# Routing groups in four classes: one half-width group, one shared condition, last stores behind it

## The chip, the cores and the metric

The kernel runs on one core of a Trainium2 chip. The core has a matrix engine (TensorE, "PE" in the profile, its weight loads "PEld"), a vector engine (VectorE, "DVE"), an activation engine (ScalarE, "ACT"), a general engine (GpSimd, "POOL") and a synchronisation engine (SyncE, "SP") that issues most transfers. Each engine runs its own list of instructions in order and waits on semaphores for the others. The metric is the device time of one execution in microseconds, the median of several; lower is better. Before the change it is 1043.65 us (three runs, 1042.89 to 1044.31).

## What is computed

There are 128 batches of 64 rows of 256 numbers. Each batch has a type label from 0 to 2 (of five experts) and goes through the dense layer of its own expert and through two shared ones; a softmax gate weighs the three results, and a diffusion step follows.

```python
def _dense(x, wi_, wo_):
    return jax.nn.relu(x @ wi_) @ wo_
x = hidden_states                                   # (128, 64, 256)
s0 = _dense(x, swi[0], swo[0])
s1 = _dense(x, swi[1], swo[1])
h = jax.nn.relu(jnp.einsum('bsd,bdf->bsf', x, wi[type_label]))   # 256 -> 1024
eo = jnp.einsum('bsf,bfd->bsd', h, wo[type_label])               # 1024 -> 256
gate_in = jnp.concatenate([eo[:, 0], s0[:, 0], s1[:, 0]], axis=-1)
w = jax.nn.softmax(jax.nn.relu(gate_in @ g1) @ g2, axis=-1)[:, :, None, None]
x = x + eo * w[:, 0] + s0 * w[:, 1] + s1 * w[:, 2]
x = x + diffusion(x, zX, zY, zR)
```

## The kernel before

**Stages.** The kernel runs two long items with the shared layers (about 0 to 90 us), five items that each take sixteen batches of one expert ("fours"), then a stage of smaller groups of batches of one expert, and then the rest of the shared layers with gate and diffusion. `stream` (L979) is the stage of smaller groups. Only this stage, the ordering of the batches ahead of it, and the seam behind it are touched.

**Groups.** `order_batches` (L256) sorts the batches on the chip by expert: small VectorE operations count them and cut each expert's count into pieces of 16, 8 and 4 batches. `GROUPS` lists the smaller ones: four groups of eight batches (512 columns) and seven of four (256 columns). The first nine (`NRUN`) always run. The last two stand under a condition each (`tc.If`, L1104), which compares the number of used slots, read from the table `tab`, with the slot at which the group starts. The labels of this input occur 43, 50 and 35 times, which fills 132 slots when each expert is rounded up to four.

**A group.** Each group loads its expert's weights (four transfers of 512 KB, tiles `gwr`) and its batches (64 KB each, `gxr`). `split_group_w` (L446) splits each eighth of the weights into a high part (ScalarE copy) and a low part (VectorE subtraction, `gw`); `split_group_x` (L438) does the same with the batches (low part on GpSimd, `gxl`). `up` (L894) multiplies: for each of eight slices f, six matmuls of the float32r type whose moving operand is as wide as the group (512 or 256 columns), each with its own weight load; then ScalarE writes the high part `gh` and VectorE the low part. `down` (L908) accumulates the second layer: for each block of 128 columns of the group and each f one matmul of 512 columns and one of 256. `store_group` (L926) adds the two halves of an accumulator (ScalarE, then VectorE, tile `ge`) and stores it to `eo_d`. For the last of the nine the store is issued on GpSimd's queue, otherwise on SyncE's.

**Order.** `ahead` (L938) places, before each slice f of group g, what belongs to later groups: their loads, their splits, the reloads `load_wo`. TensorE and SyncE keep the order in which the program is written; on ScalarE, VectorE and GpSimd a scheduler sets the order in this stage, and it is fixed once the program is built. Behind the stage the order is as written again (`in_order(True)`, L1160).

**Buffers.** Weights and wide tiles come from a pool of 25 slots (`pool4`), narrow ones from 16 (`small`), accumulators from 6 PSUM slots (`ppool`).

## Time and profile before

| what | us |
|---|---|
| median of the runs | 1043.65 |
| the profiled execution, time | 1042.87 |
| its span in the trace | 1040.7 |
| stage of the smaller groups (first `up` to the end of the last `gacc`) | 299.75 to 444.81 |
| first matmul behind the conditions | 446.55 |

The profile comes from one execution; what is counted out below is set against its span of 1040.7 us, and 2.2 us lie around that span. The median of the runs is 0.8 us above this execution's time. In the lines that follow, a matmul's duration contains its run through the array, so several in a row overlap; the distance from one to the next is (duration of the row less duration of one) divided by (count less one). "L88" is the helper that records each matmul, "L103" the helper that records each operation of VectorE, ScalarE and GpSimd, "L114" SyncE's transfers, "L1104" the condition.

### The profile page before, as it was taken

To read this page: it belongs to the slowest core of one execution; us is meant where nothing else is said; L and a number is where in the kernel's file an instruction comes from. 1 tells how busy PE (TensorE), PEld (TensorE's weight loads), DVE (VectorE), ACT (ScalarE), POOL (GpSimd) and SP (SyncE) were. 2 spreads that over 40 slices of the span, in tenths; PEclk is the share of its full clock that TensorE was granted. 3 is DMA by queue.
4 is the path that set the end of the run, shared out by engine and by line. 5 is a ranking of instruction groups with operands and counts; after the bars stand their busy time and mean duration, and the time that the engine had idled before them with its cause. 6 is when DMAs were issued, how large, how long until landed. Compare 5 with 4: busy or idle time off the path is not lost.

```text
span 1040.7 us, 15721 instructions
## 1 busy us (share of the span) xinstructions
PE 1031.7 (99%) x5439; PEld 884.7 (85%) x5439; DVE 810.3 (78%) x1492; ACT 572.5 (55%) x1081; POOL 154.4 (15%) x167
## 2 busy tenths in 40 slices
PE   9999999999999999999999999999999999999998
PEld 6888888888888889978888888888888888888888
DVE  7888987978777657847889778678688688688776
ACT  6476766766765546643644545446355364355362
POOL 2000000000022001211432220212212202022020
PEclk9999999999999999999999999999999999999999
DMA  6486232231457956555435435334344163253321
GB/s 217 178 280 234 76 112 86 95 122 52 132 192 235 320 174 213 183 183 219 156 128 177 135 111 200 122 122 167 111 167 156 66 224 122 81 192 140 115 77 47
DMA packets 67282, 159.14 MB, mean 153 GB/s; under 512 B 7712, under 2 KB 34848, under 8 KB 67200
## 3 DMA queue, kind: packets, MB, share of 16 engines
q1 hardware_dynamic: 64576, 149.19, 41.9%
q0 software_dynamic: 2480, 8.78, 2.4%
q8 instruction: 44, 0.72, 0.3%
q14 instruction: 38, 0.31, 0.1%
q10 hardware_dynamic: 144, 0.13, 0.0%
HBM read 126.88 MB, written 31.20 MB: 152 GB/s over the span
## 4 chain that ended last, share of the span: by engine, by line
PE 56%; DVE 1%; issue 0%; ACT 0%; DVEq 0%; ACTq 0%
PE acc L88 30%; PE pb L88 11%; PE pa L88 7%; PE pd L88 7%; PE pu L88 1%; DVE lq L103 0%; PE lin_b L88 0%; PE pgs L88 0%; PE lin_c L88 0%; PE pge L88 0%; DVE h_3a L103 0%; DVE c L103 0%; ACT u L103 0%; DVE pd L103 0%; DVE h_2b L103 0%
## 5 line engine op out<-in xcount | busy, mean ns | idle before, releaser
L88 PE MATMUL pb<-x,wi 128*128 128x512 f32 x729 | 207.9, 393 | 0.7 <-ACT pb L103 0.5
L103 ACT ACTIVATE u<-pb 128x512 f32<-128x512 f32 x162 | 96.8, 597 | 111.3 <-PE pb L88 109.7
L88 PEld LDWEIGHTS pb<-x,wi 128*128 128x128 f32 x729 | 130.4, 189 | 25.8 <-ACT u L103 2.4
L88 PE MATMUL pa<-x,wi 128*128 128x512 f32 x486 | 137.1, 390 | 1.7 <-DVEq L1104 1.7
L88 PE MATMUL pd<-x,wi 128*128 128x512 f32 x486 | 137.7, 392 | 0.4 <-DVE c L103 0.4
L103 DVE SCALAR_TENSOR_TENSOR yb<-acc,wgt,yb 128x256 f32<-128x256 f32 x216 | 99.2, 482 | 18.1 <-PE acc L88 14.4
L103 ACT ACTIVATE pb<-pa 128x512 f32<-128x512 f32 x81 | 47.2, 582 | 118.0 <-PE pa L88 117.0
L88 PEld LDWEIGHTS pd<-x,wi 128*128 128x128 f32 x486 | 90.9, 188 | 21.7 <-DVE c L103 1.6
L88 PEld LDWEIGHTS pa<-x,wi 128*128 128x128 f32 x486 | 89.9, 188 | 19.8 <-DVEq L1104 1.9
L103 DVE TENSOR_TENSOR c<-pd,u 128x512 f32<-128x512 f32 x81 | 55.9, 690 | 43.9 <-ACT u L103 32.7
L88 PE MATMUL up<-gxh,gw 128*128 128x256 f32 (+1 forms) x288 | 74.0, 331 | 0.0
L103 POOL TENSOR_TENSOR la<-yb 128x508 f32<-128x508 f32 (+1 forms) x28 | 32.1, 1148 | 260.9 <-ACT yb L103 259.4
L88 PE MATMUL gacc<-gw,gh 128*128 128x512 f32 (+1 forms) x288 | 62.7, 360 | 0.0
L103 ACT ACTIVATE gh<-up 128x256 fp32r<-128x256 f32 (+1 forms) x72 | 34.2, 477 | 42.9 <-PE up L88 42.0
L88 PEld LDWEIGHTS gacc<-gw,gh 128*128 128x128 f32 x288 | 49.9, 188 | 8.4
L88 PE MATMUL acc<-wo,h_6b 128*128 128x256 f32 (+1 forms) x172 | 56.7, 334 | 0.0
L88 PE MATMUL acc<-wo,h_1b 128*128 128x256 f32 (+1 forms) x172 | 56.7, 333 | 0.0
L88 PE MATMUL acc<-wo,h_7b 128*128 128x256 f32 (+1 forms) x172 | 56.6, 333 | 0.0
L88 PE MATMUL acc<-wo,h_0b 128*128 128x256 f32 (+1 forms) x172 | 56.5, 333 | 0.1
L88 PE MATMUL acc<-wo,h_2b 128*128 128x256 f32 (+1 forms) x172 | 56.6, 333 | 0.0
L88 PE MATMUL acc<-wo,h_3b 128*128 128x256 f32 (+1 forms) x172 | 56.5, 332 | 0.0
L88 PE MATMUL acc<-wo,h_4b 128*128 128x256 f32 (+1 forms) x172 | 56.5, 332 | 0.0
(251 smaller groups left out, 2476.2 us busy)
## 6 DMA issues: line engine op xcount, KB each, us to landing
wi<-wi_d SPq DMA_DIRECT2D x55, 896.0 KB, 4.6
gwr<-we_in SPq DMA_DIRECT2D x32, 512.0 KB, 5.3
wsr<-we_in SPq DMA_DIRECT2D x20, 512.0 KB, 5.5
xr<-xs_in SPq DMA_DIRECT2D x32, 256.0 KB, 5.1
yb<-xn_in SPq DMA_DIRECT2D x16, 512.0 KB, 5.9
y_out<-lq SPq DMA_DIRECT2D x30, 256.0 KB, 2.0
wi_d<-wi SPq DMA_DIRECT2D x8, 896.0 KB, 4.0
xr<-xg_in SPq DMA_DIRECT2D x80, 64.0 KB, 1.9
```

Of the source, the lines that this page charges most:

```text
L88: nc.tensor.matmul(out_ap, lhsT=lhsT, rhs=rhs, start=start, stop=stop, skip_group_check=True)
L103: ins = call(*args, **kwargs)
```

## The change

The order has four classes. Between the pieces of eight and of four it puts those pieces of four whose batches are sure to be more than two (count plus one, rounded down to four), and last the pieces that may hold only one or two batches. Of the last class the first unit (slots 128 and 129) runs at half width, two batches, as group number 3, between the third and the fourth group of eight; four units of four follow as before. The units 32 to 34 stand under one condition for all (used slots less four, or the end of the third class, over 128) and share their tiles. The stores of the last group that always runs move behind the condition, and to SyncE's queue. The half group has weights of its own to load; those of the fourth group of eight are loaded from slice 6 of the third on, and `load_wo` is spread over groups 0, 1 and 2 (3, 3 and 2).

```diff
+HALF = NBIG - 1
+UH = 2 * NPAIR + NSURE - 1
+GROUPS = [(2 * NB * g, 2 * NB) for g in range(2 * NQUAD, NPAIR)] + [(u * NB, NB) for u in range(2 * NPAIR, UH)]
+GROUPS.insert(HALF, (UH * NB, NB // 2))
+NRUN = len(GROUPS)
+GROUPS += [(u * NB, NB) for u in range(UH, NU)]
...
+        vec.tensor_scalar(cnt, pm[:, NE : 2 * NE], float(NB // 2 - 1), None, ALU.add)
+        vec.tensor_scalar(cnt, cnt, -NB, None, ALU.bitwise_and)
+        vec.tensor_copy(upto[:, 2, :], cnt)
+        vec.tensor_tensor(upto[:, 2, :], upto[:, 2, :], upto[:, 1, :], ALU.max)
...
-        for i in range(3):
+        for i in range(4):
             vec.tensor_add(rank, rank, shift[:, i, :])
...
-        vec.tensor_tensor(ge[0], ge[0], ge[1], ALU.min)
-        vec.tensor_tensor(tab[:, NSLOT : NSLOT + NU], ge[0], ge[2], ALU.min)
-        vec.tensor_copy(tab[:, NSLOT + NU :], base[0:1, 3 * NE :])
+        for i in range(1, 3):
+            vec.tensor_tensor(ge[0], ge[0], ge[i], ALU.min)
+        vec.tensor_tensor(tab[:, NSLOT : NSLOT + NU], ge[0], ge[3], ALU.min)
+        vec.tensor_scalar(gt[:, 0:1], base[0:1, 4 * NE :], float(-NB), None, ALU.add)
+        vec.tensor_tensor(tab[:, NSLOT + NU :], gt[:, 0:1], base[0:1, 3 * NE : 3 * NE + 1], ALU.max)
...
+    def own(g, key, make):
+        if g < NRUN:
+            return make()
+        if key not in spare:
+            spare[key] = make()
+        return spare[key]
...
-            if fs[-1] == NF - 1:
+            if fs[-1] == NF - 1 and g != NRUN - 1:
                 store_group(g, i)
...
-        if g == NRUN - 1:
-            tc.keep_in_program_order(nc.gpsimd.dma_start(rows, o))
-        else:
-            dma(rows, o)
+        dma(eo_d.rearrange("r (s d) -> (r s) d", d=D)[r0 : r0 + P, :], o)
...
             if g + 1 < NRUN:
-                if g < NBIG:
+                if g <= NBIG and g != HALF:
                     load_group_w(g + 1)
-                load_group_x(g + 1)
+                if g != HALF:
+                    load_group_x(g + 1)
             if g < 2:
                 reload(g)
-            elif g < 4:
-                for u in range(NQ):
-                    load_wo((g - 2) * NQ + u)
+            for u in range(3 * g, min(3 * g + 3, 2 * NQ)):
+                load_wo(u)
...
-        if f == 6 and NBIG <= g + 1 < NRUN - 1:
+        if g + 1 == HALF and f == 4:
+            load_group_x(g + 2)
+        if f == 6 and (g + 1 == HALF or NBIG <= g < NRUN - 2):
             load_group_w(g + 2)
...
+        if g == HALF + 1 and f + 6 < NF:
+            split_group_w(g, f + 6)
         if g + 1 < NRUN:
-            if f == 4:
+            if f == (0 if g == HALF else 4):
                 split_group_x(g + 1)
-            split_group_w(g + 1, f)
+            if g != HALF or f < 6:
+                split_group_w(g + 1, f)
...
-    for g in range(NRUN, NG):
-        with tc.If(total[0] > GROUPS[g][0]):
+    with tc.If(total[0] > UH * NB):
+        for g in range(NRUN, NG):
             load_group(g)
...
             stream(g, g + 1)
+    in_order(True)
+    for i in range(len(gacc[NRUN - 1])):
+        store_group(NRUN - 1, i)
```

More of the change, by code (lines that the diff above doesn't have):

```diff
@@ L28 @@
 NSURE = B // NB + 1 - 2 * NPAIR
-GROUPS = [(2 * NB * g, 2 * NB) for g in range(2 * NQUAD, NPAIR)] + [(u * NB, NB) for u in range(2 * NPAIR, NU)]
+HALF = NBIG - 1
[4 more added lines that the diff above has]
+GROUPS += [(u * NB, NB) for u in range(UH, NU)]
 NG = len(GROUPS)
-NRUN = NBIG + NSURE
 ST = 4
@@ L264, in order_batches @@
         gps.memset(ones, 1.0)
-        tables = slot2("tables")
-        below, part = (
-            tables[:, i * 9 * NE * NE : (i + 1) * 9 * NE * NE].rearrange("p (a b) -> p a b", b=3 * NE) for i in range(2)
-        )
+        tables = slot2("below"), slot2("part")
+        below, part = (t[:, 0 : 16 * NE * NE].rearrange("p (a b) -> p a b", b=4 * NE) for t in tables)
         gps.memset(below, 1.0)
         gps.affine_select(
-            out=below, in_=below, compare_op=ALU.is_ge, fill=0.0, base=0, pattern=[[1, 3 * NE], [-1, 3 * NE]],
+            out=below, in_=below, compare_op=ALU.is_ge, fill=0.0, base=0, pattern=[[1, 4 * NE], [-1, 4 * NE]],
             channel_multiplier=0,
@@ L296, in order_batches @@
         vec.tensor_scalar(cntb, cnt, -NB, None, ALU.bitwise_and)
-        size = const.tile([P, 3, NE], F32, name="size")
-        upto = const.tile([P, 3, NE], F32, name="upto")
-        vec.tensor_copy(upto[:, 2, :], cntb)
+        size = const.tile([P, 4, NE], F32, name="size")
+        upto = const.tile([P, 4, NE], F32, name="upto")
+        vec.tensor_copy(upto[:, 3, :], cntb)
         for i, n in ((1, 2 * NB), (0, 4 * NB)):
@@ L303, in order_batches @@
             vec.tensor_copy(upto[:, i, :], cntb)
+        vec.tensor_scalar(cnt, pm[:, NE : 2 * NE], float(NB // 2 - 1), None, ALU.add)
+        vec.tensor_scalar(cnt, cnt, -NB, None, ALU.bitwise_and)
+        vec.tensor_copy(upto[:, 2, :], cnt)
+        vec.tensor_tensor(upto[:, 2, :], upto[:, 2, :], upto[:, 1, :], ALU.max)
         vec.tensor_copy(size[:, 0, :], upto[:, 0, :])
-        vec.tensor_tensor(size[:, 1:3, :], upto[:, 1:3, :], upto[:, 0:2, :], ALU.subtract)
+        vec.tensor_tensor(size[:, 1:4, :], upto[:, 1:4, :], upto[:, 0:3, :], ALU.subtract)
         vec.tensor_tensor(
-            part, size.rearrange("p i e -> p (i e)").unsqueeze(1).to_broadcast([P, 3 * NE, 3 * NE]), below, ALU.mult
+            part, size.rearrange("p i e -> p (i e)").unsqueeze(1).to_broadcast([P, 4 * NE, 4 * NE]), below, ALU.mult
         )
-        base = const.tile([P, 3 * NE + 1], F32, name="base")
+        base = const.tile([P, 4 * NE + 1], F32, name="base")
         vec.memset(base[:, 0:1], 0.0)
         vec.tensor_reduce(base[:, 1:], part, AX.X, ALU.add)
-        shift = const.tile([P, 3, NE], F32, name="shift")
+        shift = const.tile([P, 4, NE], F32, name="shift")
         vec.tensor_copy(shift[:, 0, :], base[:, 0:NE])
         vec.tensor_tensor(
-            shift[:, 1:3, :], base[:, NE : 3 * NE].rearrange("p (i e) -> p i e", i=2), upto[:, 0:2, :], ALU.subtract
+            shift[:, 1:4, :], base[:, NE : 4 * NE].rearrange("p (i e) -> p i e", i=3), upto[:, 0:3, :], ALU.subtract
         )
-        vec.tensor_tensor(shift[:, 0:2, :], shift[:, 0:2, :], shift[:, 1:3, :], ALU.subtract)
-        inside = const.tile([P, 2, NE], F32, name="inside")
-        vec.tensor_tensor(inside, rank.unsqueeze(1).to_broadcast([P, 2, NE]), upto[:, 0:2, :], ALU.is_lt)
-        vec.tensor_mul(shift[:, 0:2, :], shift[:, 0:2, :], inside)
-        for i in range(3):
+        vec.tensor_tensor(shift[:, 0:3, :], shift[:, 0:3, :], shift[:, 1:4, :], ALU.subtract)
+        inside = const.tile([P, 3, NE], F32, name="inside")
+        vec.tensor_tensor(inside, rank.unsqueeze(1).to_broadcast([P, 3, NE]), upto[:, 0:3, :], ALU.is_lt)
+        vec.tensor_mul(shift[:, 0:3, :], shift[:, 0:3, :], inside)
+        for i in range(4):
             vec.tensor_add(rank, rank, shift[:, i, :])
@@ L339, in order_batches @@
         first = io[0:1, :].rearrange("p (g j) -> p g j", j=NB)[:, :, 0:1].rearrange("p g j -> p (g j)")
-        ge = [const.tile([1, NU], F32, name=f"ge{i}") for i in range(3)]
+        ge = [const.tile([1, NU], F32, name=f"ge{i}") for i in range(4)]
         gt = const.tile([1, NU], F32, name="gt")
-        cmp = tables[0:1, 0 : NU * (NE - 1)].rearrange("p (g e) -> p g e", e=NE - 1)
-        for i in range(3):
+        cmp = tables[0][0:1, 0 : NU * (NE - 1)].rearrange("p (g e) -> p g e", e=NE - 1)
+        for i in range(4):
             b = base[0:1, i * NE + 1 : i * NE + NE]
@@ L366, in clear_spare @@
         gps.memset(zero, 0.0)
-        r0, r1 = GROUPS[NRUN][0] * NT, NSLOT * NT
+        r0, r1 = UH * NB * NT, NSLOT * NT
         for r in range(r0, r1, P):
@@ L372, in cond_resid_kernel @@
     graw, gw, gxr, gx, gval = {}, {}, {}, {}, {}
+    spare = {}
+    def own(g, key, make):
[4 more added lines that the diff above has]
+        return spare[key]
     def group_tile(g, shape, dtype, name):
-        pool, tag = (pool4, "t4") if g < NBIG else (small, "s2")
-        return pool.tile(shape, dtype, tag=tag, name=name)
+        pool, tag = (pool4, "t4") if GROUPS[g][1] > NB else (small, "s2")
+        return own(g, name, lambda: pool.tile(shape, dtype, tag=tag, name=f"{name}{g}"))
     def load_batches(s0, n, dst):
@@ L384, in load_batches @@
             )
-            for j in range(NB):
+            for j in range(min(NB, n)):
                 dma(dst(j0 + j), xg[bass.ds(vals[j], 1), :, :].rearrange("o p k -> p (o k)"))
@@ L389, in load_group_x @@
         s0, n = GROUPS[g]
-        xr = gxr[g] = group_tile(g, [P, n, 2 * S], F32, f"gxr{g}")
+        xr = gxr[g] = group_tile(g, [P, n, 2 * S], F32, "gxr")
         load_batches(s0, n, lambda j: xr[:, j, :])
@@ L421, in load_group_w @@
         for h in range(NQ):
-            r = slot4(f"gwr{g}_{h}", F32)
+            r = own(g, ("raw", h), lambda: slot4(f"gwr{g}_{h}", F32))
             dma(r, we[bass.ds(gval[g], 1), :, 2 * h : 2 * h + 2, :].rearrange("o p f c -> p (o f) c"))
@@ L438, in split_group_x @@
     def split_group_x(g):
-        hi = group_tile(g, [P, 2, GROUPS[g][1], S], F32R, f"gxh{g}")
-        lo = group_tile(g, [P, 2, GROUPS[g][1], S], F32R, f"gxl{g}")
+        hi = group_tile(g, [P, 2, GROUPS[g][1], S], F32R, "gxh")
+        lo = group_tile(g, [P, 2, GROUPS[g][1], S], F32R, "gxl")
         src = gxr.pop(g).rearrange("p j (k s) -> p k j s", k=2)
@@ L446, in split_group_w @@
     def split_group_w(g, f):
-        w = slot4(f"gw{g}_{f}")
+        w = own(g, ("w", f), lambda: slot4(f"gw{g}_{f}"))
         split(w[:, 0, :], w[:, 1, :], graw[g, f], vec)
@@ L895, in up @@
         w, (xh, xl), cols = gw[g, f], gx[g], GROUPS[g][1] * S
-        ps = (seeded if f % 2 and cols == 512 else psum)(f"up{g}_{f}")
+        ps = own(g, ("up", f % 2), lambda: (seeded if f % 2 and cols == 512 else psum)(f"up{g}_{f}"))
         todo = [(k, wp, xx) for k in range(2) for wp, xx in ((0, xh), (0, xl), (1, xh))]
@@ L899, in up @@
             mm(ps[:, :cols], w[:, wp, k * P : (k + 1) * P], xx[:, k, :], i == 0, i == len(todo) - 1)
-        hi = slot2(f"gh{g}_{f}", F32R)
+        hi = own(g, ("h", f), lambda: slot2(f"gh{g}_{f}", F32R))
         lo = slot2(f"gl{g}_{f}", F32R) if cols == 512 else hi[:, 256:512]
@@ L913, in down @@
         if fs[0] == 0:
-            gacc[g] = [ppool.tile([P, 2, D], F32, tag="ps", name=f"gacc{g}_{i}") for i in range(m)]
+            gacc[g] = [
+                own(g, ("acc", i), lambda: ppool.tile([P, 2, D], F32, tag="ps", name=f"gacc{g}_{i}")) for i in range(m)
+            ]
         for i in range(m):
@@ L920, in down @@
                 mm(gacc[g][i][:, 0, :], h[j][1][:, i * P : (i + 1) * P], w[j][:, 0, 256:512], False, f == NF - 1)
-            if fs[-1] == NF - 1:
+            if fs[-1] == NF - 1 and g != NRUN - 1:
                 store_group(g, i)
-        if fs[-1] == NF - 1:
-            del gacc[g]
     def store_group(g, i):
         acc = gacc[g][i]
-        o = small.tile([P, D], F32, tag="s2", name=f"ge{g}_{i}")
+        o = own(g, ("o", i), lambda: small.tile([P, D], F32, tag="s2", name=f"ge{g}_{i}"))
         act.activation(o, acc[:, 0, :], AF.Copy)
@@ L931, in store_group @@
         r0 = GROUPS[g][0] * S + i * P
-        rows = eo_d.rearrange("r (s d) -> (r s) d", d=D)[r0 : r0 + P, :]
-        if g == NRUN - 1:
-            tc.keep_in_program_order(nc.gpsimd.dma_start(rows, o))
-        else:
-            dma(rows, o)
+        dma(eo_d.rearrange("r (s d) -> (r s) d", d=D)[r0 : r0 + P, :], o)
     def ahead(g, f):
@@ L1158, in sums @@
         return join(*(at(k + i, w) for i, w in enumerate(work)))
-    in_order(True)
     left = [], []
```

## The prediction

> **What bounds the kernel now.** I read the page first: the engines' shares, then the chain that ended last.

> ```profile
> PE 1031.7 (99%) x5439; PEld 884.7 (85%) x5439; DVE 810.3 (78%) x1492; ACT 572.5 (55%) x1081; POOL 154.4 (15%) x167
> PEclk9999999999999999999999999999999999999999
> PE 56%; DVE 1%; issue 0%; ACT 0%; DVEq 0%; ACTq 0%
> ```

> TensorE works 99% of the span at the full granted clock. The chain is TensorE's own work, followed back 594 us to the seam behind the smaller groups (56% and 1%); there it begins with a wait. A change is worth what it takes from TensorE's list, and costs what makes TensorE wait. Next I cut the stage of the smaller groups by group (columns: stretch, its length, busy time of PE, PEld, DVE, ACT, POOL, then clock, share of the transfer engines, GB/s).

> ```profile
> 343.60:365.60 22.00, 22.00 (x113) 18.82 (x112) 12.86 (x23) 11.91 (x23) 2.42 (x1) 1.00 0.89 322
> 365.60:387.50 21.90, 21.90 (x118) 18.97 (x118) 12.09 (x22) 10.76 (x22) 1.29 (x1) 1.00 0.59 204
> 387.50:399.00 11.50, 11.50 (x83) 10.77 (x82) 8.92 (x19) 8.04 (x20) 1.30 (x1) 1.00 0.57 172
> 399.00:410.50 11.50, 11.50 (x84) 10.80 (x83) 8.18 (x18) 8.35 (x20) 1.29 (x1) 1.00 0.70 225
> ```

> A group of eight takes 22, a group of four 11.4 us, with TensorE never idle. VectorE has 3 us to spare in a group of four, and the transfers are near their limit in the third group of eight (0.89). The third view is TensorE's order of time, for the distance between matmuls.

> ```profile
> 441.49 0.19 PEld L88 LDWEIGHTS up<-gxl,gw 128*128 128x128 f32 x1
> 441.61 0.19 PEld L88 LDWEIGHTS up<-gxh,gw 128*128 128x128 f32 x1
> 305.22 1.98 PE L88 MATMUL gacc<-gw,gh 128*128 128x512 f32 x8
> 469.46 0.54 PEld L88 LDWEIGHTS pl<-g2t,gh 128*128 128x128 f32 x4
> 469.58 0.51 PE L88 MATMUL pl<-g2t,gh 128*128 128x3 f32 x4
> 449.47 1.98 PEld L88 LDWEIGHTS pgs<-gis,g1t 128*128 128x128 f32 x16
> ```

> Loads for float32r matmuls of 256 columns come 0.12 us apart (441.49, 441.61), as their matmuls do (0.119 over eight); eight of 512 columns take (1.98 - 0.39)/7 = 0.227 each. The four `pl` matmuls move 3 columns and still come (0.54 - 0.19)/3 = 0.117 apart: that is a weight load of 128 columns of four bytes. The last view is the seam.

> ```profile
> 441.85 2.96 PE L88 MATMUL gacc<-gw,gh 128*128 128x512 f32 x16
> 446.55 0.98 PE L88 MATMUL pa<-x,wi 128*128 128x512 f32 x3 [1.74 <-DVEq L1104]
> 442.46 0.42 DVE L103 SCALAR_TENSOR_TENSOR gh<-up,gh 128x256 fp32r<-128x256 f32 x1 [0.29 <-ACT gh L103]
> 445.03 0.76 DVE L103 TENSOR_TENSOR ge<-gacc,ge 128x256 f32<-128x256 f32 x2 [2.14 <-ACT ge L103]
> 450.30 1.05 POOL L458 DMA_INDIRECT eog<-eo_d,gone  x1 [2.44 <-ACT u L103]
> ```

> TensorE ends at 444.81 and idles 1.74 us: VectorE first finishes the evacuation `ge` (445.79) and then needs 0.76 us for two conditions.

> **The change, part by part.**

> *The half group.* It replaces a group of four: 48 matmuls of 256 columns, 16 of 512, 16 of 256, by my distances 48 x 0.119 + 16 x 0.227 + 16 x 0.119 = 11.24 us (seen: 11.4). At half width it has 48 of 128 columns, 8 of 512 and 8 of 256. The trace has no float32r matmul of 128 columns. From below, pure streaming at half of 0.119 would be 0.06; but each matmul here brings its own weights, and the `pl` row shows that these alone take 0.117. From above, `pgs` is plain float32 of the same 128 columns: 16 loads at (1.98 - 0.19)/15 = 0.119, two to a call, 0.24 us a call. I take 0.117: the 256-column matmuls of the same type come at their streaming distance, so nothing but the weight load should stand under them. Half group: 48 x 0.117 + 8 x 0.227 + 8 x 0.119 = 8.38 us, a gain of 2.86. So a half group is no half: its first layer keeps its price. Bounds: 48 x 0.06 gives a gain of 5.6, 48 x 0.24 a loss of 3.0.

> [...]

> *What waits in the half group.* VectorE's order in the built program is fixed: between the four evacuations `ge` of the third group of eight and the eviction `gh` of slice 5 of the half group stand eight weight splits, two of the fourth group of eight and six already of the group after it, and three evictions. In the trace splits in a row (0.68 long) start 0.60 apart, a `ge` 0.34, and an eviction of 128 columns, from 0.42 at 256 and 0.69 at 512, is 0.28, about 0.2 apart. That is 4 x 0.34 + 8 x 0.60 + 4 x 0.2 + about 0.3 for waits = 7.3 us. TensorE needs in the same time: four narrow matmuls (0.5), slices 2 to 7 of `up` (36 x 0.117 = 4.2), two `down` steps (2 x 0.69), the wide part of the third (0.46), 6.5 us, and starts some 0.4 us earlier. So it waits about 1.2 us at the narrow part of slices 4 and 5; the evictions of slices 6 and 7 stand behind on VectorE, but TensorE wants those only after two slices of the next group (2.7 us). From below: 0, if VectorE starts early enough; from above: with 0.773 a split (the group's mean in the profile, which holds those slowed by GpSimd) 8 x 0.17 = 1.4 more, 2.6. I take 1.2.

> *Transfers.* Until the end of the third group of eight, the core now loads 2 MB more of weights (the half group's), 0.13 MB of its batches, and 2 MB more of `wo`: about 4 MB over 66 us, on a use of 216, 265 and 322 GB/s. That fills the transfer engines. Cover: on SyncE the fourth group's weights have only its batches ahead of them, slice 6 of the third group lies 5.5 us before its end, and their splits spread over the 8 us behind that; the median landing of such a load is 5.3 us, the worst in this crowded stretch 7.5. Price 0; if the cover is gone, VectorE stands at a split, the evictions behind it are late, TensorE waits: up to 4 us, if the transfers move only 250 GB/s there (4 MB x (1/250 - 1/330) = 3.9).

> *The seam.* The evacuation now stands behind the condition. VectorE's last operation ahead of its branch is the eviction that ended at 442.88, 1.9 us before TensorE's last matmul, so its branch is hidden. The 1.74 us go. TensorE's own branch now stands in the middle of its last matmuls: 0 if it reads ahead, at most 0.76; I take 0.35, half of VectorE's two. Next in line: ScalarE's two `ge` (0.66) come before the copy of `pa`, which needs 0.98 us of matmul first, so they hide. The two stores go to SyncE, where nothing else is due until 454.84, and land 1.8 us on; the gather `eog` on GpSimd can go at 3 us after TensorE's end instead of 5.5, and its reader on TensorE (456.49, 9.9 us after the first matmul) still has 7 us, against the 6.2 that sufficed. Price 0.

> *The ordering.* Eleven more small VectorE operations at 0.2 us apart, and two that grow from 225 to 400 elements (0.39 to about 0.57): 2.5 us, at 40 to 50 us of the span, where VectorE is busy 7.3 of 8 us. The four us behind it leave 1.3 free. So up to 1.2 us reach TensorE through `c` and `h`; at the least 0. I take 0.45, since TensorE runs ahead of them. The larger table fill on GpSimd (0.56 us at 225) and a second clearing store are hidden: GpSimd is idle there.

> The condition is not taken: 132 used slots less 4 is 128, and the third class ends at 128. The half group's shorter evictions save ScalarE and VectorE work that does not bind.

> Sum: -2.86 + 1.2 - 1.74 + 0.35 + 0.45 = -2.6 us. Span 1040.7 to 1038.1; against the median 1043.65 to 1041.05, say 1041.0.

> **The rivals.**

> *Narrow float32r matmuls are slow (slower).* Place: the 48 `up` matmuls of the half group. For it: the only 128-column calls in the trace, `pgs`, cost 0.24; against: they are plain float32, sent as two instructions each, and float32r at 256 columns shows no such halving of speed. At 0.24 the group lasts 48 x 0.24 + 2.77 = 14.3, 3.05 more than the group of four; VectorE then has time, so no 1.2; with the seam and the ordering +2.1 us: 1045.8, slower by just over 0.2%. It turns into a loss from 48u + 2.77 - 11.24 - 0.94 = 0, u = 0.196 us a matmul on.

> *The transfers are full.* For it: 0.89 and 322 GB/s in the third group; against: the landings. With 2 to 4 us of waiting: 1043 to 1045.

> *More than I count.* No wait in the half group, and a hidden branch: -2.86 - 1.74 + 0.45 = -4.15, 1039.5. For it: the 1.2 is the difference of two long sums.

> *It does not tell.* The half group's stall at its upper end (2.6) and the ordering at 1.2: -0.5 us, 1043.2.

> **How the numbers follow.** Forecast 0.43, more 0.13, slow matmuls 0.27 (the only 128-column calls on record are slow ones, so this is no small chance; by 0.23 us or less, where the time is still within 0.2%, four tenths of it), transfers 0.09, no difference 0.08. The range 1039.3 to 1046.2 runs from the case of more to the slow one, whose 1045.8 gets 0.4 of the ordering's upper end, and leaves 2 in 10 out. A measurement of this kernel can tell about 0.2%, 2.1 us, from no change: 1041.56 to 1045.74. My forecast lies only 0.5 us beyond the border, so of its 0.43 I put 0.32 on faster; with the case of more 0.45. Slower: 0.16 of the slow matmuls and 0.03 of the transfers, 0.19. The rest, 0.36, is no difference.

> **What would show it.** The 128x128 `up` rows at 0.117 us apart and the half group at 8.4 us plus a wait of about 1.2 at `gacc` released by VectorE; the first `pa` at most 0.4 us behind the last `gacc`; a first `up` 0.3 to 0.6 us later than 299.75; everything behind the seam unchanged. Wrong would be: `up` rows at 0.2 or more; waits on `gwr` in the third group of eight; a new wait at the gate's reader `pt_e`.

## The result and the profile after

The changed kernel takes 1041.05 us (median of 14, 1040.44 to 1043.03) against 1043.64 before (14 runs): ratio 0.9975, 95% interval 0.9967 to 0.9984. Measured once more at the end, it took 1042.09 against 1043.09, ratio 0.9989 (0.9978 to 1.0000); the last experiment shows where that comes from. The profiled execution has a span of 1039.9 us (time 1041.6), the one before 1040.7 (1042.87).

The forecast was 1041.0. The total came out as forecast, but not all of its terms: one was wrong by 1.9 us. First, two lines of the page, the engines' busy time and the chain that ended last.

```profile
PE 1030.5 (99%) x5423; PEld 882.1 (85%) x5423; DVE 810.6 (78%) x1502; ACT 571.5 (55%) x1080; POOL 154.3 (15%) x165
...
PE 57%; DVE 0%; ACT 0%; issue 0%; DVEq 0%
```

TensorE is as full as before, and the chain is still its own work. The view of TensorE's waits (who waited for whom, us in total, times, longest):

```profile
PE gacc L93 <- PEq L1124: 2.0, 1, 2.0
...
PE gacc L93 <- DVE gh L108: 0.9, 1, 0.9
PE acc L93 <- DVE h_6b L108: 0.6, 1, 0.6
```

The wait on L1104 is gone from the list. Two others are new in it: 2.0 us on TensorE's own sequencer ("PEq") at the new condition, L1124, and 0.9 us on the eviction `gh`. The third, 0.6 on `h_6b`, lies at 83.9 us, behind the ordering. Next the stage by group (columns as before the change; the third group of eight, the half group and the fourth of eight, cut at the first `up` of each).

```profile
342.51:364.56 22.05, 22.05 (x114) 18.84 (x113) 12.24 (x22) 12.69 (x25) 3.41 (x2) 1.00 0.75 271
364.56:376.01 11.45, 10.54 (x78) 9.64 (x77) 9.62 (x24) 7.62 (x22) 0.00 (x0) 1.00 0.76 245
376.01:395.97 19.96, 19.96 (x101) 17.00 (x101) 11.44 (x18) 9.65 (x18) 1.31 (x1) 1.00 0.60 195
```

The transfers are no limit: 0.75 in the third group of eight, where they stood at 0.94 before, cut the same way (341.06 to 363.12 us; the prediction's cut, 2.5 us later, had 0.89). The second group of eight is the fullest now, with 0.87, and no wait on `gwr` reaches TensorE. The half group's stretch (which still holds the last two accumulator steps of the group ahead of it) is the only one in which TensorE idles. Its order of time there, and VectorE's:

```profile
373.30 0.39 PE L93 MATMUL up<-gxh,gw 128*128 128x128 f32 x2
373.53 0.28 PE L93 MATMUL up<-gxl,gw 128*128 128x128 f32 x1
373.64 0.38 PE L93 MATMUL up<-gxh,gw 128*128 128x128 f32 x2
373.86 0.28 PE L93 MATMUL up<-gxl,gw 128*128 128x128 f32 x1
373.97 0.28 PE L93 MATMUL up<-gxh,gw 128*128 128x128 f32 x1
374.09 0.80 PE L93 MATMUL gacc<-gw,gh 128*128 128x512 f32 x3
375.79 0.39 PE L93 MATMUL gacc<-gw,gh 128*128 128x256 f32 x1 [0.91 <-DVE gh L108]
```

```profile
368.61 1.42 DVE L108 TENSOR_TENSOR ge<-gacc,ge 128x256 f32<-128x256 f32 x4 [1.83 <-ACT ge L108]
369.95 0.69 DVE L108 TENSOR_TENSOR gw<-gwr,gw 128x512 fp32r<-128x512 f32 x1
...
370.85 1.28 DVE L108 TENSOR_TENSOR gw<-gwr,gw 128x512 fp32r<-128x512 f32 x2
...
372.25 1.89 DVE L108 TENSOR_TENSOR gw<-gwr,gw 128x512 fp32r<-128x512 f32 x3
...
374.25 1.28 DVE L108 TENSOR_TENSOR gw<-gwr,gw 128x512 fp32r<-128x512 f32 x2
375.45 0.68 DVE L108 SCALAR_TENSOR_TENSOR gh<-up,gh 128x128 fp32r<-128x128 f32 x3
```

The narrow matmuls start 0.11 us apart (373.53 to 373.97: four steps, 0.44). All 48, each to the next start, take 5.16 us, 0.1075 each. VectorE runs without a gap from the four `ge` at 368.61 through eight splits; only then, at 375.45, comes the eviction of slice 5, and TensorE's accumulator step waits until 375.79. The seam in TensorE's order of time:

```profile
441.31 1.80 PE L93 MATMUL gacc<-gw,gh 128*128 128x512 f32 x9
445.13 1.41 PE L93 MATMUL gacc<-gw,gh 128*128 128x512 f32 x7 [2.02 <-PEq L1124]
446.38 0.85 PE L93 MATMUL pa<-x,wi 128*128 128x512 f32 x3
```

The first `pa` now follows the last `gacc` after 0.12 us. But 2 us of idle time stand ahead of the last seven `gacc`. The view of the condition's line has TensorE's branch (count; shortest/median/longest in ns; first and last start):

```profile
L1124 PEldq COMPARE_BRANCH  x1: 3734/3734/3734, 441.2 to 441.2; - x1
```

It lasts 3.73 us. In the kernel before, TensorE's two branches, and the first instructions behind each, were these, and VectorE (446.55) was later than all of them:

```profile
L1104 PEldq COMPARE_BRANCH  x2: 219/288/358, 442.9 to 445.0; - x2
L1104 PEldq EVENT_SEMAPHORE  x2: 51/51/51, 444.9 to 445.3; - x2
```

### The profile page after: what moved, and what is told of

It is laid out like the page before. It is cut to its first block, busy times and chain, and to the rows that moved or that the text cites. A ratio compares the mean times of both kernels' runs of the same rounds, so it can differ in the third digit from the quotient of the medians.

```text
span 1039.9 us, 15667 instructions
## 1 busy us (share of the span) xinstructions
PE 1030.5 (99%) x5423; PEld 882.1 (85%) x5423; DVE 810.6 (78%) x1502; ACT 571.5 (55%) x1080; POOL 154.3 (15%) x165
## 4 chain that ended last, share of the span: by engine, by line
PE 57%; DVE 0%; ACT 0%; issue 0%; DVEq 0%
PE acc L93 30%; PE pb L93 11%; PE pd L93 7%; PE pa L93 7%; PE pu L93 1%; PE lin_b L93 0%; PE pgs L93 0%; PE gacc L93 0%; PE lin_c L93 0%; PE pge L93 0%; DVE lq L108 0%; DVE c L108 0%; ACT pb L108 0%; DVE end_qb L108 0%; PE pl L93 0%
## 5 line engine op out<-in xcount | busy, mean ns | idle before, releaser
L108 DVE SCALAR_TENSOR_TENSOR yb<-acc,wgt,yb 128x256 f32<-128x256 f32 x216 | 99.3, 482 | 18.1 <-PE acc L93 14.3
L93 PE MATMUL up<-gxh,gw 128*128 128x512 f32 (+2 forms) x288 | 73.4, 329 | 0.0
L93 PEld LDWEIGHTS gacc<-gw,gh 128*128 128x128 f32 x272 | 47.4, 188 | 11.6 <-issue 2.3
L108 DVE TENSOR_TENSOR gw<-gwr,gw 128x512 fp32r<-128x512 f32 x72 | 53.1, 780 | 5.0 <-ACT gw L108 4.9
L93 PE MATMUL acc<-wo,h_5b 128*128 128x256 f32 (+1 forms) x172 | 56.5, 332 | 0.0
```

Of the source, the lines that this page charges most:

```text
L93: nc.tensor.matmul(out_ap, lhsT=lhsT, rhs=rhs, start=start, stop=stop, skip_group_check=True)
L108: ins = call(*args, **kwargs)
```

## The experiments

### What the branch costs

`e2`: one condition for each seldom unit.

```diff
-    with tc.If(total[0] > UH * NB):
-        for g in range(NRUN, NG):
+    for g in range(NRUN, NG):
+        with tc.If(total[0] > GROUPS[g][0]):
```

> The changed kernel with one condition for each of the three seldom units instead of one for all three: three jumps over about 160 TensorE instructions each instead of one over 480. Theory (TensorE's 2.02 us at the condition is the fetch of code at a far jump target): each branch lasts 0.2 to 0.4 us as the two in the kernel before did, the idle time at the condition falls to 0 to 0.7 us, and the time falls by 1.3 to 2 us, to 1039.0 to 1039.8. Rival (each condition costs TensorE some 2 us wherever it stands among its matmuls): three of them make it 4 to 6 us of idle time, and 1043 to 1045 us.

Measured: 1041.16 us, ratio to before 0.9981 (0.9972 to 0.9990), no different from the changed kernel. Its waits and, from the view of the condition's line, its branches:

```profile
PE gacc L93 <- PEq L1125: 1.7, 1, 1.7
```

```profile
L1125 PEldq COMPARE_BRANCH  x3: 219/358/962, 440.4 to 442.9; - x3
```

Two of the three rows are short, as my theory had it (the third lasts 0.96 us), and yet the time doesn't fall: from the first branch (440.41) to the instruction behind the third (443.93) pass 3.5 us, against 3.8 in one jump (441.23 to 445.02). So "short jumps are cheap" falls, and so does "each condition costs 2 us", which asked for 4 to 6 us of idle time. What is left is that the price goes with the code passed, in however many jumps; the two jumps of the kernel before took 2.4 (442.94 to 445.35).

`e5` has one unit behind the condition, `e6` no unit and no condition. Both leave out units that don't run for this input.

```diff
-        for g in range(NRUN, NG):
+        for g in range(NRUN, NRUN + 1):
```

> The changed kernel with only the first seldom unit under its condition (the other two, which don't run for this input, are left out): TensorE jumps over about 160 instructions instead of 480. Theory (the price is the code that the jump passes: 3.7 us from the branch to the next instruction for 480, 2.08 for the first 160 of the run with three conditions, and 1.75 us of matmuls that TensorE had read ahead hide part of it): idle time at the condition 0.3 to 0.4 us instead of 2.0, time 1.6 to 1.9 us less than the changed kernel's 1041.05: 1039.2 to 1039.4. Rival (a taken branch costs TensorE the same whatever it passes): idle 2.0, 1041.

> The changed kernel with the condition and the three seldom units left out altogether (they don't run for this input). Theory: the 2.0 us of idle time among the last accumulator matmuls goes and nothing takes its place, the first pa follows at once: 1041.05 less 2.2, 1038.8; this is the most that any cheaper condition can bring. Rival (another wait stands right behind, such as the copy that the first pb needs, or the gate's gather): 0.5 to 1 us of it come back, 1039.5.

Measured: `e5` 1038.93 us (0.9954, 0.9939 to 0.9969), `e6` 1038.41 (0.9949, 0.9934 to 0.9964). The last accumulators in `e5`'s order of time, its branch, and the same place in `e6`:

```profile
443.12 3.35 PE L93 MATMUL gacc<-gw,gh 128*128 128x512 f32 x16
```

```profile
L1124 PEldq COMPARE_BRANCH  x1: 349/349/349, 443.0 to 443.0; - x1
```

```profile
441.18 2.97 PE L93 MATMUL gacc<-gw,gh 128*128 128x512 f32 x16
443.99 0.86 PE L93 MATMUL pa<-x,wi 128*128 128x512 f32 x3
```

Sixteen accumulator matmuls take 2.97 us with no condition, 3.35 past 160 instructions, and 5.23 in the changed kernel (441.31 to 446.54). The jump over one unit still takes 2.0 us to the next instruction (443.04 to 445.04); the matmuls that TensorE had read ahead (in the changed kernel nine, 1.80 us from 441.31 on, with the branch at 441.23) hide all but 0.4 of it. The 480 instructions cost 2.3 us, and nothing stands behind: `e6` gains 2.6 us by the medians. The rival, a fixed price of a taken branch, falls with `e5`. Nor is it the place of the branch in the code: in `e3` below TensorE has 32 instructions more ahead of it, and idles 2.0 us again.

The trace also lists the transfers of code: the page counts, on queue q8 of the kind `instruction`, 44 packets with 0.72 MB, 16 KB each. Set against TensorE's 10,846 instructions that is some 247 to a packet, so I take this queue for TensorE's. In the changed kernel such a packet starts 1.0 us behind the branch (442.22) and lasts 1.4 us. In `e5` one starts as late behind it and ends at 445.04, when the next instruction starts. From `e5` (160 instructions, 2.0 us) to the changed kernel (480, 3.8 us) the price grows with the code passed; `e2` (three jumps of 160, 3.5 us) says that the number of jumps isn't what counts. Why more code passed costs more no run shows.

`e9`: all three units under one condition, and a hint that names the branch's target, four slices ahead.

```diff
+        if g == NRUN - 1 and f == 4:
+            with tc.issue_after(last_mm[0].ins):
+                tc.mark_branch_hint_location("seldom", engines=(mybir.EngineType.PE,))
...
-    with tc.If(total[0] > UH * NB):
+    with tc.If(total[0] > UH * NB, label="seldom"):
```

> The changed kernel with all three seldom units under the one condition, and one instruction more on TensorE: a hint, four slices (about 6 us) ahead of the branch, that names the branch's target as the code to fetch. Theory (the 2.0 us are the fetch of the target's code): with the target fetched ahead, the branch costs 0.3 to 0.5 us to the next instruction, which the matmuls already read ahead hide; idle time there under 0.5, time near the 1038.4 of the kernel without a condition, 1038.4 to 1039.2. Rival (the hint isn't followed, or it displaces the code that TensorE needs next): 1041.05 as before, or an idle place of 1 to 4 us before the branch and up to 1043.

Its order of time at the seam, then the rows of its branch and of the hint from the views of their lines:

```profile
441.16 1.80 PE L95 MATMUL gacc<-gw,gh 128*128 128x512 f32 x9
443.11 1.41 PE L95 MATMUL gacc<-gw,gh 128*128 128x512 f32 x7
```

```profile
L1129 PEldq COMPARE_BRANCH  x1: 392/392/392, 441.1 to 441.1; - x1
```

```profile
L1278 PEldq BRANCH_PREFETCH_HINT  x1: 45/45/45, 434.3 to 434.3; - x1
```

The branch over the same 480 instructions takes 0.39 us, the next instruction comes 1.9 us behind it, and the 16 accumulator matmuls take 3.36 us, as in `e5`. The only change is that the target is named early, and a 16 KB packet more starts 1.3 us behind the hint; so I take the 1.9 us that went (of 3.8) for the fetch of the target's code. One packet still starts 1.1 us behind the branch, and what the remaining 1.9 us consist of is not shown. The time, 1040.43 us (0.9968, 0.9956 to 0.9980; six runs, 1038.98 to 1041.51), is 1.2 us above the range I expected, so by itself it doesn't show the gain; those six runs scatter by 2.5 us. `e10` and `e12` below, with the same hint and two more edits, repeat the seam of this profile and are 2.5 and 3.0 us below the changed kernel where its clock holds.

### What the narrow group is worth

`e3`: the half group at full width (`NB // 2` becomes `NB` in `GROUPS.insert`; its two more slots are empty).

> The changed kernel with the half-width group widened to four batches (its two more slots are empty ones of this input), all else kept: order in four classes, one condition, stores behind it. Theory: TensorE works 2.65 us longer there, the 0.9 us wait on VectorE at the group's fourth accumulator step goes, so +1.7 us: 1042.8; 256-column rows 0.119 apart in place of 0.109. Rival (the stall moves rather than goes, since VectorE has the same splits to do): +2.65, 1043.7. If the narrow group were worth nothing, 1041.0.

Measured: 1043.32 us, ratio to before 1.0006 (0.9997 to 1.0015). From the first `up` to the last `gacc` the profile has 147.05 us against 145.07: the half width is worth 2.0 us net of its wait (which is gone here, as the theory said), and 2.3 by the medians. With the full width the change brings nothing: seam and ordering together are no gain.

`e7`: the splits placed in the half group cut from six to four.

```diff
-        if g == HALF + 1 and f + 6 < NF:
-            split_group_w(g, f + 6)
+        if g == HALF + 1 and f + 4 < NF:
+            split_group_w(g, f + 4)
...
-            if g != HALF or f < 6:
+            if g != HALF or f < 4:
```

> The changed kernel with four instead of six weight splits of the fourth group of eight placed in the half-width group; the other two move into that group itself. Theory (the 0.9 us wait at the group's accumulator is VectorE's fixed order: eight splits ahead of one eviction, 0.6 us each): two fewer make its list 1.2 us shorter, the wait is gone or under 0.1, 1041.05 less 1.1, 1040.0. Rival (the wait goes to the next place, since VectorE has the same splits to do): a wait of half a us or more in the first slices of the fourth group of eight, 1040.6 to 1041.

The half group's last accumulators in its order of time:

```profile
373.96 0.95 PE L93 MATMUL gacc<-gw,gh 128*128 128x512 f32 x3
375.19 0.39 PE L93 MATMUL gacc<-gw,gh 128*128 128x256 f32 x1 [0.28 <-DVE gh L108]
```

The wait shrinks from 0.91 to 0.28 and comes back nowhere in the fourth group of eight, but it doesn't go: the scheduler took only one split of eight out of the way. The stage is 0.6 us shorter. The median, 1041.33 (0.9973, 0.9963 to 0.9984), doesn't show it: in 5 of the 12 executions the mean granted clock is 0.998, which is taken up at the end of this section. The other seven have a median of 1040.31, 0.7 below the changed kernel.

### The ordering

`e4` is the kernel before with the longer ordering alone, `e8` the changed kernel with the table built in nine fewer VectorE operations (two classes to a comparison). `e1` is the kernel before once more.

> The kernel before with nothing but the changed kernel's longer ordering (ten more small VectorE operations and the larger tables; its third class is set so that the fourth is empty, which gives the order of the kernel before). Theory (the ordering delays TensorE by about 1.4 us, as the two profiles show at the groups' start): first group at 300.8 to 301.3, time +1.0 to +1.5, 1044.6 to 1045.1. Rival (the prediction's 0.45, the rest being scatter of single executions): 1044.1. Rival (nothing reaches TensorE): 1043.65.

> The changed kernel with the ordering's table built in fewer VectorE operations (the comparisons for two classes at a time; nine fewer operations in all), same result. Theory (the longer ordering reaches TensorE: from the first pb to the first group 279.65 us in the runs with it against 278.5 without): that distance falls to 278.6 to 279.0, time 0.6 to 1.0 us less, 1040.1 to 1040.5. Rival (what counts is not the operations' number but the scatter of these stretches): 279.65 again, 1041.05.

> The kernel before, unchanged, a second time, for its median span and for how much its waits differ from one execution to the next. Theory: the profiled execution shown first (span 1040.7) is a usual one, so the first matmul of the groups starts again near 299.75 us, the idle time at the conditions is again 1.7, and the time behind the seam again 594.2; the median span is then about 1041.5 (1043.65 less 2.2). Rival: the terms behind the result scatter by half a us or more from one execution to the next; then the first group's start, or the time behind the seam, lies 0.5 us or more elsewhere, and comparing two single profiles says little about terms of this size.

Measured: `e4` 1043.75 us (1.0004, 0.9995 to 1.0013), `e8` 1041.07 (0.9978, 0.9969 to 0.9987), `e1` 1043.58 (0.9999, 0.9990 to 1.0008). From the first `pb` to the first `up` of the groups the profiles have 278.35 and 278.73 us in two executions of the kernel before; 279.12 to 279.77 in the nine runs with the longer ordering, among them 279.43 in `e4` and 279.77 in the changed kernel; and 278.52 to 278.93 in the three with the shorter table, 278.85 in `e8`. The means are 278.5, 279.5 and 278.8. So ten more small operations cost TensorE about 1.0 us in the profiles, and the shorter table gives 0.7 back. Of this, 0.7 repeats from run to run: the matmul that comes 220 behind the first `pb` starts 42.97 to 43.03 us behind it in the kernel before and with the shorter table, and 43.59 to 43.74 with the longer ordering. The rest lies in waits at `pb` and `acc` near 74 and 83 us, which vary between 0 and 0.7 us from profile to profile.

The medians show less. `e4` is 0.2 us above `e1`, nearer to "nothing reaches TensorE" than to its theory, and `e8` is no faster than the changed kernel; their intervals are 0.9 us to either side and allow 1.0 as well as 0. Terms under 1 us are below what they resolve. `e1` tells why: the first `pb` itself starts at 21.40 us in one execution of the kernel before and at 22.06 in the other (20.87 to 23.64 over all profiles), and the span is 1041.7 instead of 1040.7, while the idle time at the conditions (1.7) and the time behind them (589.8 to the last matmul) repeat within 0.05. So `e1`'s rival held for the start of the program, and its theory for the seam and what follows.

### Together, and the changed kernel again

`e10` and `e12` are one kernel: the hint, `e7`'s splits and `e8`'s table. `e11` is the changed kernel, on the same chip as `e12`.

> The hint, the later splits and the shorter table in one kernel. If the three gains add up: the hint's -2.0 to -2.6, the splits' -0.5 (the narrow group's wait was 0.3 instead of 0.9 in the profile), the table's -0.5 to -0.8 from the first pb to the first group: 1037.2 to 1038.2. If only the hint's counts, as the medians of the two others say: 1038.4 to 1039.0. If the hint does nothing: 1040 to 1041.

> The changed kernel, unchanged, once more, beside the kernel before and the next one on the same chip. The terms read off the profiles so far (narrow group -3.15 and its wait +1.16, wait behind the seam -1.9, TensorE's branch +2.26, ordering about +1.0, behind the seam -0.6) sum to -1.2 us; the medians said -2.6. Theory that the count of the profiles is complete: 1042.2 to 1042.6, ratio 0.9987. Rival (the profiled executions of before and after were not typical, the start of the program scatters): 1041.0 to 1041.5 again, ratio 0.9975 to 0.9980, and the profile shows the same stage and seam (145.1 us from the first up to the last gacc).

> The hint, the later splits and the shorter table in one kernel, once more, on the same chip as the changed kernel. If its advantage is real: 2.2 to 3.0 us below the changed kernel of this call, 5 us below the kernel before (ratio 0.995 to 0.9965). If the five executions before were lucky: 1.0 to 2.0 below the changed kernel.

Measured: `e10` 1038.58 us (0.9958, 0.9945 to 0.9971), `e12` 1038.03 (0.9953, 0.9940 to 0.9966), `e11` 1042.09 (0.9989, 0.9978 to 1.0000). In the profiles the gains add up: from the first `up` of the groups to the first `pa` behind them both take 142.84 us, the changed kernel 145.19, near the hint's 1.9 (2.3 less the 0.4 that stays) and the splits' 0.6; the table gives 0.7 ahead of that. The times agree less closely. `e10` lies 2.5 us below the first measurement, in the range expected for the hint alone; `e12` lies 4.1 below `e11`, and 3.0 below those executions of `e11` whose clock held. So the sum of about 3.2 is not contradicted, but not measured apart from the hint either. The waits of `e12`, where no condition stands any more, and its seam in order of time:

```profile
PE gacc L95 <- DVE gh L110: 0.3, 1, 0.3
```

```profile
439.32 3.35 PE L95 MATMUL gacc<-gw,gh 128*128 128x512 f32 x16
```

This kernel is 5 us faster than the one before, and it keeps all seldom units, so it beats both.

`e11` gave the ratio of the first theory and the stage of the second, so neither held as written. What differs is the clock (stretches of 4 us at the seam of `e11`; the column behind POOL is the granted clock):

```profile
440.00:444.00 4.00, 2.64 (x18) 2.14 (x16) 0.85 (x2) 0.77 (x2) 0.00 (x0) 1.00 0.03 8
444.00:448.00 4.00, 3.57 (x15) 2.90 (x16) 0.88 (x3) 1.24 (x3) 0.00 (x0) 0.73 0.12 39
448.00:452.00 4.00, 4.00 (x24) 3.54 (x24) 1.38 (x3) 1.20 (x2) 2.00 (x2) 0.84 0.21 62
```

From 445.9 to 449.3 us the granted clock is one half, and everything behind the seam is late by 1.2 us (590.67 us from the first `pa` to the last matmul, 589.47 in the first profile). In 8 of `e11`'s 12 executions the mean clock is 0.998, and in 1 of the 14 executions of the first measurement; such a stretch alone takes 0.0016 from the mean, and the one other profile with 0.998, `e7`, has it too (from 445.6 us). The executions without it have a median of 1041.03 here and 1041.05 there; those of the kernel before, 1043.17 (69 of 95). So the change is worth 2.1 us where the clock holds, and what it brings in the median depends on how often the clock drops behind the idle time of 2 us, which it keeps.

## Why the forecast came out, term by term

The terms as measured, in us, from start to start of matmul records in the two profiles first shown; the ordering is from the means above.

| step | forecast | measured |
|---|---|---|
| half group, matmuls | -2.86 | -3.15 |
| half group, wait | +1.2 | +1.16 |
| wait behind the last `gacc` | -1.74 | -1.90 |
| TensorE's branch | +0.35 | +2.26 |
| ordering | +0.45 | about +1.0 |
| behind the seam | 0 | -0.36, and -0.23 at the end |
| sum | -2.6 | -1.2 |

**Narrow matmuls: right, and the rival of slow ones falls.** 0.1075 instead of 0.117 us each; 240 `up` matmuls of 256 columns took 28.67 us, the 192 that are left and the 48 narrow ones take 28.10. The first layer indeed keeps its price; the accumulators' -2.78 are the gain, less 0.2 at four changes of width. The `pl` row, a load of four-byte weights (0.117), was the right neighbour, and the plain float32 `pgs` (0.24 a call) the wrong one.

**The wait: right in place, releaser and size.** I worked out 7.3 us for VectorE from the first `ge` to the eviction of slice 5; it took 7.1 (368.61 to 375.74). TensorE's accumulator step takes 1.92 us to the next `up` (374.09 to 376.01), the step before it, without a wait, 0.76: that is the 1.16. The eight splits are the 39th to 46th of the program's 72. At eight to a group, these are the last two of the fourth group of eight and six of the group after it, as the prediction had it.

**Where it failed: TensorE's own branch, "0 if it reads ahead, at most 0.76".** I took the upper bound from VectorE's two branches and applied it to TensorE, whose skipped code is far longer. The kernel before had the evidence: behind TensorE's first branch (442.94) the next instruction came only at 444.85. It was hidden, because the evacuation on VectorE was later still, and I read the visible wait as the only one. That removing VectorE's wait uncovers TensorE's is what the section on the seam should have asked under "next in line". The seam, forecast at -1.39, is +0.36.

**The ordering was too small by half** if the profiles are right, and its bound of 1.2 about right; the medians of `e4` and `e8` do not exclude 0.45. The first `up` came 1.4 us later than before (301.19), where I had said 0.3 to 0.6. There are ten more operations, not eleven.

**Behind the seam** I expected nothing. In all kernels with the changed seam the wait for `c` 107 us behind it is 0.27 us shorter, and the way from the last matmul to the end takes 0.23 less in the profile shown first (0.1 to 0.7 less in the others). I have not settled why.

**Why the total agrees.** The branch and the ordering cost 2.5 us more than forecast, and 1.1 us of other terms went better (0.3, 0.16 and 0.6), so the terms sum to -1.2, half the forecast. The medians lie nearer to it: -2.1 where the clock holds, and -2.6 in the first measurement, in which the clock dropped in 1 of 14 executions of the changed kernel and (over all measurements) in 26 of 95 of those before. So the forecast hit partly by luck. Between -1.2 and -2.1, 0.9 us are open. The two profiles first shown are not typical: the span of the kernel before (1040.7) is 0.6 us below the median span of its 69 executions whose clock held (1041.3), and that of the changed kernel (1039.9) 0.6 above its own (1039.3). The idle time at the new condition is 2.02 us there and 1.75 to 2.00 in `e2`, `e3`, `e7`, `e8` and `e11`, and of the ordering's 1.0 only 0.7 repeats; together these can hold up to 0.6 of the 0.9. Where the rest lies no run shows. The rival with full transfers falls (no wait on `gwr` reaches TensorE; share 0.75 in the third group of eight), and so does the new wait at the gate's reader.

## What to carry to other kernels

When a wait at a condition is taken from one engine, look at when each other engine's next instruction behind its branch comes; here the one that was second took its place (2.0 us on TensorE after 1.74 on VectorE). The engine with the longest skipped code paid most (TensorE's branch 3.73 us, VectorE's 0.07). Naming the target ahead of the branch took 1.9 us of idle time away, keeping less code behind it as much; moving stores and evictions around the condition had gained nothing. The group at half width saved little in its first layer (0.1075 us a matmul of 128 columns against 0.119 of 256, where the weight loads of the `pl` row alone come 0.117 apart); its second layer, whose matmuls keep their width, halved (2.78 us less, of the 5.5 that 16 matmuls at 0.227 and 16 at 0.119 take).

## What the hardware showed that I had not expected

In `e7` and `e11` an idle time of 1.8 us on TensorE was followed by a granted clock of one half for 3.4 us, from 1.2 to 1.4 us after TensorE had started again (from 445.6 and 445.9 us), which cost 1.2 us in `e11`. The mean clock is 0.998 in 51 of 178 executions of the kernels whose idle time at the seam is 1.7 us or more, and in none of 28 of those whose idle time there is 0.4 or less (`e5`, `e6`, `e9`, `e10`, `e12`). In the changed kernel's first profile an idle time of 2.0 us left the clock whole. What decides between them is not shown.
